# Queries and keys by seven half-size products, and one order for all block stages

## The chip, the cores and the metric

The kernel runs on one core of a Trainium2 chip. A core has a matrix engine (PE, with its weight loads listed apart as PEld), a vector engine (DVE), an activation engine (ACT), a third vector engine (POOL) and one that issues most of the DMAs (SP). Each takes its own instructions in the order in which they were written; semaphores tie them together. Matmul results land in PSUM, and DVE or ACT must read them out before the buffer can be used again.

The metric is the device time of one launch in microseconds, lower is better; the time of a kernel is the median of its runs.

## The reference

Two batches of 1024 tokens with 512 features, all fp32. After a layernorm there are two branches, and their product is added to the input.

```python
x = L0_attn_x                      # (2, 1024, 512)
xn = _layernorm(x, axis=-1)
# attention: 32 heads of 16, causal
q = (xn @ Wq.T + bq).reshape(b, l, h, hd).transpose(0, 2, 1, 3)
k = (xn @ Wk.T + bk).reshape(b, l, h, hd).transpose(0, 2, 1, 3)
v = (xn @ Wv.T + bv).reshape(b, l, h, hd).transpose(0, 2, 1, 3)
scores = jnp.einsum('bhqd,bhkd->bhqk', q, k) / math.sqrt(hd)
att = jax.nn.softmax(jnp.where(causal, scores, -jnp.inf), axis=-1)
s = jnp.einsum('bhqk,bhkd->bhqd', att, v).transpose(0, 2, 1, 3).reshape(b, l, d) @ Wo.T + bo
# gate: a base projection and two of eight rank-16 experts, chosen by a softmax
result = jnp.einsum('bnd,od->bno', xn, W_base) + b_base
g = _silu(result + delta * SCALING)
x = x + s * g
```

## The kernel before

The tokens of a batch are cut into two chunks of C = 512 (c = 0, 1), the features into KC = 4 blocks of 128 (oc). A *unit* (b, oc, c) is the attention of one chunk of queries for the eight heads of one block: 2 x 4 x 2 = 16 units. A unit of c = 0 has 5 steps and one of c = 1 has 13, since it looks back at the first chunk too: 144 steps in all, the list `plan`. The order of the units is by batch, block and chunk, with a few neighbours swapped, so that units of c = 0 often follow one another.

A step n writes, in this order: `scores(n)` (line 1218: matmuls of 32 rows side by side, then two exponentials of 128x1024 on ACT, line 1236), `values(n - 1)` (the product of the exponentials of the step before with v, line 1272), `masked(n)` (DVE multiplies the diagonal blocks of the exponentials by the causal mask), and `fill(n)`. At the end of a unit DVE copies two results, and `post` starts a chain of small DMAs and DVE operations (den, dens, rc, back, rb) that divides by the sums of the softmax.

`fill(n)` (line 1150) is a planner that runs while the program is written. All other work is a list of tasks, each with a due step, a cost in PE time (MM = 0.853 us by its own estimate, the time of 512 columns through 128 rows for all 128 outputs), conditions, and rooms (counts of free buffers) that it takes and frees. The planner takes matmul tasks in order of due step until the step has its even share of the remaining cost; tasks without matmuls (layernorm, sums, combining of weights) go where its estimate of DVE's time leaves room, or when they are due. So the order on every engine is settled before the kernel runs.

Products come in three forms. `matmul` (line 216) writes every product as four column groups of 32 outputs, which PE runs side by side; all of them are recorded at line 219.

- Queries and keys: `qk_task` (line 375) multiplies a block of weights (128 features out) with the 512 tokens of a chunk, four products of 128 rows and 512 columns for q and four for k. ACT reads q out twice (once for each parity of heads, line 388) and k once (line 402). The weights wq_sb and wk_sb are loaded once, 128 columns at a time, and stay in SBUF.
- Values, gate and output projections: `block_task` (line 515) computes a 512 by 512 product in blocks of 256, by seven block products in place of eight (Strassen's scheme in Winograd's form). For that `sums_task` (line 503) makes four sums of blocks of the tokens on DVE, and `combine_task` (line 459) four sums of blocks of the weights once, which go to DRAM (`kept`). The weight parts come back one by one into six buffers (`issue_parts`, tag wp). The ten such products are the `stages`, and stage k + 1 begins its sums only when stage k has ended.
- The first unit, the routing and the end have forms of their own.

PSUM has two buffers of tag mm for all these products, so a product can begin only when the one before the last has been read out. The sums of the tokens have one buffer (tag sums), taken from the beginning of a stage's sums to its end.

Of the kernel before, what the change touches and what calls it, by code (L numbers as in the profile page):

```python
# [8 lines left out]
F32 = mybir.dt.float32  # L9
# [8 lines left out]
P = 128  # L18
# [62 lines left out]
def direct(ctx, tc, sound, x, wq, wk, wv, wo, wb, wa, wg, wB, bq, bk, bv, bo, bb, out):  # L81
# [34 lines left out]
    def load_w(src, cols, name, o0=0):  # L116
        t = cst.tile([P, KC, cols], F32, name=name)
        nc.sync.dma_start(
            out=t, in_=src.rearrange("(kc p) o -> p kc o", p=P)[:, :, o0 : o0 + cols]
        )  # L120
        return t
# [15 lines left out]
    wq_sb = [load_w(wq, P, "wq_sb0")]  # L137
    wk_sb = [load_w(wk, P, "wk_sb0")]
    wv_sb = load_whole(wv, "wv")
    bv_sb = load_b(bv, "bv_sb")  # L140
    for oc in range(1, KC):
        wq_sb.append(load_w(wq, P, f"wq_sb{oc}", oc * P))
        wk_sb.append(load_w(wk, P, f"wk_sb{oc}", oc * P))
# [30 lines left out]
    bq_half = cst.tile([P, 2, KC], F32, name="bq_half")  # L174
    mhalf = cst.tile([P, 1], F32, name="mhalf")
# [130 lines left out]
    def first_task():  # L306

        xnT = sb.tile([P, KC, C], F32, tag="xnT", bufs=3, name="xnT_0_0")
        qT = sb.tile([P, 2, C], F32, tag="qT", bufs=3, name="qT_0_0_0")
        kT = sb.tile([P, C], F32, tag="kT", bufs=4, name="kT_0_0_0")  # L310
        xnTs[0, 0], qTs[0, 0, 0], kTs[0, 0, 0] = xnT, qT, kT
        pq = ps_av.tile([P, C], F32, tag="av", name="pq_first")
        pk = ps_av.tile([P, C], F32, tag="av", name="pk_first")

        def turn(t):
            pt = mm_tile("pt_x")
            for k in range(KC):
                nc.tensor.transpose(
                    pt[:, k * P : (k + 1) * P], first[t][:, k * P : (k + 1) * P], ident
                )  # L320
            nc.scalar.copy(
                xnT[:, :, t * P : (t + 1) * P], pt.rearrange("p (k t) -> p k t", k=KC)
            )
            turned_at[0, 0] = now[0] - 5

        def project_first(ps, w, t):
            cols = slice(t * P, (t + 1) * P)
            for k in range(KC):
                nc.tensor.matmul(  # L329
                    ps[:, cols], lhsT=w[:, k, :], rhs=xnT[:, k, cols], start=k == 0, stop=k == KC - 1  # L330
                )

        def queries(par):
            ve.tensor_scalar(
                qT[:, par], pq, bq_sb[:, 0:1], half[:, par : par + 1], ALU.add, ALU.mult
            )

        def keys(t0, t1):
            cols = slice(t0 * P, t1 * P)
            nc.scalar.activation(kT[:, cols], pk[:, cols], AF.Identity, bias=bk_sb[:, 0:1])  # L340

        def transform(t, s):
            normalize(first[t : t + 1], *s)
            turn(t)

        s0 = yield from statistics(first[0 : 1])
        s1 = yield from statistics(first[1 : 2])
        transform(0, s0)
        b_ps = mm_tile("b_ps")[:, 0 : 2 * KC]
        nc.tensor.transpose(b_ps, b_rows, ident[0 : 2 * KC, 0 : 2 * KC])  # L350
        nc.scalar.copy(b_sb, b_ps)
        s2 = yield from statistics(first[2 : 3])
        transform(1, s1)
        project_first(pq, wq_sb[0], 0)
        s3 = yield from statistics(first[3 : 4])
        transform(2, s2)
        project_first(pk, wk_sb[0], 0)
        transform(3, s3)
        room["x"] += 1
        keys(0, 1)  # L360
        project_first(pq, wq_sb[0], 1)
        project_first(pq, wq_sb[0], 2)
        project_first(pq, wq_sb[0], TT - 1)
        queries(0)
        queries(1)
        for par in range(2):
            ve.tensor_scalar(bq_half[:, par], bq_sb, half[:, par : par + 1], None, ALU.mult)
        project_first(pk, wk_sb[0], 1)
        yield 6 * MM
        project_first(pk, wk_sb[0], 2)  # L370
        project_first(pk, wk_sb[0], 3)
        keys(1, TT)
        yield 2 * MM

    def qk_task(b, oc, c):
# [4 lines left out]
        for k in range(KC):  # L380
            matmul(
                pq, lhsT=wq_sb[oc][:, k, :], rhs=xnT[:, k, :], start=k == 0, stop=k == KC - 1
# [12 lines left out]
        for k in range(KC):  # L395
            matmul(
                pk, lhsT=wk_sb[oc][:, k, :], rhs=xnT[:, k, :], start=k == 0, stop=k == KC - 1
# [5 lines left out]
        kTs[b, oc, c] = kT  # L403
        yield MM
# [25 lines left out]
    def v_task(b, i):  # L430
# [17 lines left out]
    PARTS = ("11", "t2", "21", "t3", "t1", "22", "t4")  # L448
    weights = {"v": (wv, bv_sb), "gate": (wb, bb_sb), "out": (wo, bo_sb)}
    stages = (  # L450
        [("v", 0, 1), ("gate", 0, 0), ("gate", 0, 1), ("v", 1, 0), ("out", 0, 0), ("v", 1, 1)]
        + [("out", 0, 1), ("gate", 1, 0), ("gate", 1, 1), ("out", 1, 0)]
    )
    parts = [(k, j) for k in range(len(stages)) for j in range(len(PARTS))]
    NWP = 6
    places, used, issued = {}, [0], [0]
    combined, kept_at, b_diff, sums, sums_at, issued_at, ended = {}, {}, {}, {}, {}, {}, [0]

    def combine_task(name, given=None):
# [5 lines left out]
        at = lambda i, j: w[:, 2 * i : 2 * i + 2, BK * j : BK * j + BK]  # L465
        s = sb.tile([P, 4, 2, BK], F32, tag="sums", bufs=1, name="wsum")
        ve.tensor_tensor(s[:, 0], at(0, 1), at(0, 0), ALU.subtract)
        ve.tensor_tensor(s[:, 1], at(1, 1), s[:, 0], ALU.subtract)
        yield WAIT
        ve.tensor_tensor(s[:, 2], at(1, 1), at(0, 1), ALU.subtract)  # L470
        ve.tensor_tensor(s[:, 3], at(1, 0), s[:, 1], ALU.subtract)
        kept = dram.tile([P, 4, 2, BK], F32, tag=f"kept_{name}", bufs=1, name="kept")
        nc.sync.dma_start(out=kept, in_=s)
# [4 lines left out]
        for _ in range(1 if given else 2):  # L478
            yield WAIT

    def issue_parts():
        while issued[0] < len(parts) and issued[0] - used[0] < NWP:
# [6 lines left out]
            if part[0] == "t":  # L489
                src = combined[name][:, int(part[1]) - 1]  # L490
# [6 lines left out]

    def tokens(k):
        name, b, c = stages[k]
# [3 lines left out]
    def sums_task(k):  # L503
        at = tokens(k)
        s = sb.tile([P, 4, 2, BK], F32, tag="sums", bufs=1, name="asum")
        ve.tensor_tensor(s[:, 0], at(1, 0), at(1, 1), ALU.add)
        yield PAUSE
        ve.tensor_tensor(s[:, 1], s[:, 0], at(0, 0), ALU.subtract)
        sums[k], sums_at[k] = s, now[0]
        yield PAUSE  # L510
        ve.tensor_tensor(s[:, 2], at(0, 0), at(1, 0), ALU.subtract)
        yield PAUSE
        ve.tensor_tensor(s[:, 3], at(0, 1), s[:, 1], ALU.subtract)

    def block_task(k, slot, final, more=None):

        name, b, c = stages[k]
        at, s = tokens(k), sums[k]
# [13 lines left out]
        def product(name, a):  # L532
            ps = mm_tile(name)
            part = k, used[0] - k * len(PARTS)
# [15 lines left out]
            used[0] += 1  # L550
            if not closes:
# [7 lines left out]
        add(s11, p1, like(s11, bias[:, 0:BK]))  # L559
        yield MM  # L560
        p6 = yield from product("p6", s[:, 1])
        add(s12, p6, s11)
        yield MM
        p2 = yield from product("p2", at(0, 1))
        add(s11, p2, s11)
        final(0, 0)
        yield MM
        p7 = yield from product("p7", s[:, 2])
# [4 lines left out]
        p5 = yield from product("p5", s[:, 0])  # L573
# [5 lines left out]
        p3 = yield from product("p3", s[:, 3])  # L579
# [11 lines left out]
        final(1, 0)  # L591
        ended[0] += 1
# [372 lines left out]
    units[-3], units[-2] = units[-2], units[-3]  # L965

    for n in (1, 2 * KC + 1):
# [8 lines left out]
    room = {"x": 1, "xnT": 2, "qT": 3, "kT": 4, "v": 3, "hl": 1, "hwT": 2, "g": 2, "sums": 1}  # L976
# [46 lines left out]
    def stage(task, what, due, cost, takes, uses, ready, frees=()):  # L1023

        k = stages.index(what)
        Task(
            due - 8 if k else -9, sums_task(k), 0.0, takes={"sums": 1},
            ready=lambda: ended[0] == k and ready(),
        )
        Task(  # L1030
            due, task(k), cost, takes=takes, uses=uses, frees={"sums": 1, **dict(frees)},
            ready=lambda: now[0] > sums_at.get(k, now[0]) and issued_at.get((k, 1), now[0]) < now[0],
        )

    tasks = []
    for b in range(NB):
        for c in range(NC):
# [11 lines left out]
            for oc in range(KC):  # L1049
                if oc or b or c:  # L1050
                    Task(
                        starts[b, oc, c] - 1, qk_task(b, oc, c), 8 * MM, takes={"qT": 1, "kT": 1},
                        uses=xn,
                        ready=lambda u=units[units.index((b, oc, c)) - 1], t=turned_: u in qk_begun
                        and t(),
                    )
            if not b and not c:
                room["v"] -= 1
                for t in range(TT):
# [5 lines left out]
                    3, combine_task("v", wv_sb), 0.0, after=5, takes={"sums": 1},  # L1065
                    frees={"sums": 1}, uses=[("xnT", "wv")],
                )
                for n, name in enumerate(("gate", "out")):
                    Task(
                        16 + n, combine_task(name), 0.0, after=9, takes={"sums": 1, "xnT": 1},  # L1070
                        frees={"sums": 1, "xnT": 1}, ready=lambda n=n: ended[0] > 0 and len(combined) > n,
                    )
            else:
                stage(values_task, ("v", b, c), s0 + (5 if c else 1), 14 * MM, {"v": 1}, xn, turned_)
            done = starts[b, KC - 1, c] + len(unit_steps(c))
            Task(
                done - (16 if (b, c) != (NB - 1, NC - 1) else 36), route_task(b, c), TT * KC * MM * (ER + E) / D, takes={"hl": 1}, uses=xn,
# [3 lines left out]
                done - (14 if (b, c) != (NB - 1, NC - 1) else 34), routed_task(b, c), 0.0, takes={"hwT": 1}, frees={"hl": 1},  # L1081
# [6 lines left out]
            if (b, c) != (NB - 1, NC - 1):  # L1088
                by = min(len(plan) - 3, done + (21 if c else 19 if b else 16))
# [4 lines left out]
            else:  # L1094
# [23 lines left out]
                )  # L1118
    tasks.sort(key=lambda x: x.due)
# [661 lines left out]
```

## Time and profile before

| | us |
|---|---|
| median of 3 runs | 611.37 (611.22 to 611.74) |
| profiled execution, whole | 612.12 |
| its span, first to last instruction | 610.4 |
| exponentials on ACT, line 1236, 288 of 1021 ns | 279.1 busy |
| pq and pk, 480 matmul records each, 592 ns | 56.6 and 56.6 busy |
| products of 256 columns, p<-wt,asum, 960 records, 379 ns | 58.0 busy |
| DVE's masks, 90 of 690 ns and 76 of 421 ns | 61.2 and 30.8 busy |
| ACT qT<-pq, 30 of 774 ns, and kT<-pk, 15 of 687 ns | 21.7 and 10.3 busy |
| bytes moved by DMA | 52.30 MB, mean 86 GB/s |

The granted clock of PE was 0.997. Busy times of PE count a stretch once even where four column groups run in it; the mean of one record is longer than the time until the next, because records overlap. So the price of a piece of work on PE is better read from the start of one step to the start of the next than from the records' means.

### The profile page before, as it was taken

Reading aid. Unit: us, or ns where it says so; the run is one execution under the profiler, and the core shown is the slowest. Engines: PE = TensorE matmul, PEld = TensorE weight load, DVE = VectorE, ACT = ScalarE, POOL = GpSimd, SP = SyncE. Lnnn points to the kernel's source line nnn. Section 1 sums busy time; section 2 is a strip of 40 time slices with the busy share of each in tenths; the row PEclk is TensorE's granted clock in tenths of the full one; section 3 lists DMA queues with packets and bytes.
Section 4 is the critical chain, followed back from the end, with each engine's and each line's share of the span. In section 5 each row is a group of like instructions: output and inputs, shape, how many; then the busy total and the mean of one; then the engine's idle time right before and its main releaser. Section 6 shows DMA issues by size and latency. Waiting matters only on the chain.

```text
span 610.4 us, 17914 instructions
## 1 busy us (share of the span) xinstructions
PE 599.4 (98%) x7991; PEld 265.4 (43%) x7991; DVE 346.2 (57%) x710; ACT 328.0 (54%) x381; POOL 8.9 (1%) x26
## 2 busy tenths in 40 slices
PE   8999999999999999999999999999999999999995
PEld 8335343423443244434344443452355444347662
DVE  4546664362298227856279644554349854766733
ACT  2435446566556655655545555446655655665351
POOL 2100000000000000000000000000000000000000
PEclk9999999999999999999999999999999999999998
DMA  9824315320521325025134121340112213401201
GB/s 270 180 70 141 113 55 175 119 91 19 130 59 46 106 54 124 22 72 183 46 100 133 39 73 57 103 124 4 35 37 74 58 40 101 163 19 41 72 20 57
DMA packets 47428, 52.30 MB, mean 86 GB/s; under 512 B 8056, under 2 KB 34688, under 8 KB 46960
## 3 DMA queue, kind: packets, MB, share of 16 engines
q1 hardware_dynamic: 47328, 51.08, 28.1%
q8 instruction: 64, 1.05, 0.7%
q14 instruction: 20, 0.16, 0.1%
q10 hardware_dynamic: 16, 0.00, 0.0%
HBM read 39.05 MB, written 12.03 MB: 84 GB/s over the span
## 4 chain that ended last, share of the span: by engine, by line
PE 95%; DVE 1%; DMA 1%; ACT 1%; issue 0%; SPq 0%; DVEq 0%
PE s L1227 25%; PE av L1272 23%; PE p L219 21%; PE pk L219 8%; PE pq L219 8%; PE pv L219 2%; PE ph L219 2%; PE po L219 2%; ACT pt L1236 1%; DMA x<-in_x_dram 1%; DMA dens<-den 1%; PE pq_first L329 1%; PE h L219 1%; PE pk_first L329 0%; DVE x L55 0%; DVE y L55 0%
## 5 line engine op out<-in xcount | busy, mean ns | idle before, releaser
L1236 ACT ACTIVATE pt<-s 128x1024 f32<-128x1024 f32 x288 | 279.1, 1021 | 210.6 <-PE s L1227 208.5
L1227 PE MATMUL s<-qT,kT 32*128 32x512 f32 (+3 forms) x1824 | 166.5, 464 | 0.1
L55 DVE TENSOR_TENSOR pt<-pt,causal 128x256 f32<-128x256 f32 (+1 forms) x166 | 92.1, 567 | 131.1 <-ACT pt L1236 130.9
L1272 PE MATMUL av<-pt,v 128*32 128x512 f32 (+3 forms) x1824 | 154.0, 443 | 0.6 <-DVE avs L55 0.6
L1227 PEld LDWEIGHTS s<-qT,kT 32*128 32x128 f32 x1824 | 72.9, 184 | 87.6 <-issue 40.5
L1272 PEld LDWEIGHTS av<-pt,v 128*32 128x32 f32 x1824 | 43.1, 109 | 89.4 <-issue 60.8
L219 PE MATMUL p<-wt,asum 128*32 128x256 f32 x960 | 58.0, 379 | 0.0
L219 PE MATMUL pk<-xnT,wk_sb 128*32 128x512 f32 x480 | 56.6, 592 | 0.0
L219 PE MATMUL pq<-xnT,wq_sb 128*32 128x512 f32 x480 | 56.6, 592 | 0.0
L219 PEld LDWEIGHTS p<-wt,asum 128*32 128x32 f32 x960 | 31.1, 110 | 27.8 <-issue 10.5
L55 DVE TENSOR_TENSOR g<-p,g 128x512 f32<-128x512 f32 x28 | 18.9, 687 | 21.7 <-PE p L219 21.4
L388 ACT ACTIVATE qT<-pq,bq_half,half 128x512 f32<-128x512 f32 x30 | 21.7, 774 | 14.4 <-PE pq L219 14.4
L219 PEld LDWEIGHTS pk<-xnT,wk_sb 128*32 128x32 f32 x480 | 15.5, 110 | 31.6 <-issue 31.1
L219 PEld LDWEIGHTS pq<-xnT,wq_sb 128*32 128x32 f32 x480 | 15.4, 110 | 29.1 <-issue 28.1
L219 PE MATMUL p<-w,xnT 128*32 128x256 f32 x448 | 26.7, 379 | 0.0
L55 DVE TENSOR_TENSOR v<-p,v 128x512 f32<-128x512 f32 x21 | 14.2, 689 | 19.3 <-PE p L219 19.1
L626 ACT ACTIVATE sg<-g 128x512 f32<-128x512 f32 x16 | 10.1, 630 | 21.1 <-DVE g L55 21.1
L219 PE MATMUL p<-w,asum 128*32 128x256 f32 x320 | 20.6, 379 | 0.0
L219 PEld LDWEIGHTS p<-w,xnT 128*32 128x32 f32 x448 | 14.4, 110 | 12.0 <-issue 4.8
L55 DVE TENSOR_TENSOR x<-p,x 128x512 f32<-128x512 f32 x21 | 14.1, 685 | 7.5 <-PE p L219 7.4
L219 PE MATMUL ph<-wag_sb,xnT 128*32 128x136 f32 x512 | 17.9, 280 | 0.3
L219 PEld LDWEIGHTS ph<-wag_sb,xnT 128*32 128x32 f32 x512 | 14.9, 110 | 7.1 <-issue 5.4
(122 smaller groups left out, 416.8 us busy)
## 6 DMA issues: line engine op xcount, KB each, us to landing
wt<-kept SPq DMA_DIRECT2D x40, 256.0 KB
x<-in_x_dram SPq DMA_DIRECT2D x16, 256.0 KB
scr<-sq SPq DMA_DIRECT2D x6, 512.0 KB
xnT<-scr SPq DMA_DIRECT2D x24, 128.0 KB
kept<-wsum SPq DMA_DIRECT2D x3, 1024.0 KB
w<-in_wb_dram SPq DMA_DIRECT2D x12, 256.0 KB
xr<-in_x_dram SPq DMA_DIRECT2D x12, 256.0 KB
out_dram<-x SPq DMA_DIRECT2D x12, 256.0 KB
```

Source lines behind the costliest of these rows:

```text
L55: return getattr(self.engine, name)(*args, **named)
L219: nc.tensor.matmul(o[j : j + 32], lhsT=lhsT[:, j : j + 32] if len(lhsT.shape) == 2 else lhsT[:, j // 32], rhs=rhs, start=start, stop=stop,)
L329: nc.tensor.matmul(ps[:, cols], lhsT=w[:, k, :], rhs=xnT[:, k, cols], start=k == 0, stop=k == KC - 1)
L388: nc.scalar.activation(qT[:, par], pq, AF.Identity, bias=bq_half[:, par, oc : oc + 1], scale=half[:, par : par + 1],)
L626: nc.scalar.activation(sg, g(i, j), AF.Tanh, scale=0.5)
L1227: nc.tensor.matmul(ss[s // 2][:, s % 2, col : col + w], lhsT=kT[rows, kt % TT * P : kt % TT * P + P], rhs=qTs[b, oc, c][rows, par, q0 : q0 ...
L1236: nc.scalar.activation(pt[:, 2 * pair : 2 * pair + 2], ss[pair], AF.Exp, scale=0.25)
L1272: nc.tensor.matmul(avs_now[par][32 * s : 32 * s + 32, q0 : q0 + w], lhsT=vs[b, kt][:, h * VS - HD * par : h * VS - HD * par + HP], rhs=pt[ ...
```

## The change

Thirteen of the sixteen units now get their queries and keys from `qk_blocks_task`. It puts the two weight blocks side by side as one 512 by 256 operand (128 outputs for q, 128 for k) and computes both by the same seven-product scheme: seven products with 256 rows and 256 tokens each, in place of eight with 128 rows and 512 tokens. The results are added up by DVE, eight operations of 128x256 a unit, in place of ACT's three reads; the biases enter there (`b_less` is bq - bk). ACT then makes the two parities of q from the finished tile, one step later.

The first unit and the two that follow it keep their old products. The weight blocks are loaded into two buffers in turn (`load_qk`), for each batch anew; `qk_weights_task` makes the weights' sums in the first batch, keeps them in DRAM, and fetches them in the second.

All block stages, those of q and k among them, stand in one list of groups and run in this order. Stages of one group use the same tokens and share one set of four token sums, which now have a buffer each; a sum for the next group may be written once the product that last reads the old one has been issued. The products of a stage come in another order (the two plain ones first), and `combine_task` writes the weights' sums in place. The due steps follow: no stage is due later than the one after it. Two neighbouring units of the first batch swap places, and routing and gate tasks are due at other steps.

```diff
+    def load_qk(oc):
+        t = sb.tile([P, 4 * KC, P], F32, tag="wqk", bufs=2, name=f"wqk{oc}")
+        for n, src in enumerate((wq, wk)):
+            nc.sync.dma_start(
+                out=t[:, n * KC : n * KC + KC],
+                in_=src.rearrange("(kc p) o -> p kc o", p=P)[:, :, oc * P : oc * P + P],
+            )
...
-    PARTS = ("11", "t2", "21", "t3", "t1", "22", "t4")
+    PARTS = ("11", "21", "t2", "t3", "t1", "22", "t4")
-    stages = (
-        [("v", 0, 1), ("gate", 0, 0), ("gate", 0, 1), ("v", 1, 0), ("out", 0, 0), ("v", 1, 1)]
-        + [("out", 0, 1), ("gate", 1, 0), ("gate", 1, 1), ("out", 1, 0)]
+    groups = (
+        [("v", 0, 1), ("qk", 0, 1, 1)],
+        [("gate", 0, 0), ("qk", 0, 0, 2), ("qk", 0, 0, 3)],
+        [("qk", 0, 1, 2), ("gate", 0, 1), ("qk", 0, 1, 3)],
+        [("v", 1, 0), ("qk", 1, 0, 0), ("qk", 1, 0, 1)],
+        [("out", 0, 0)],
+        [("qk", 1, 1, 0), ("v", 1, 1), ("qk", 1, 1, 1)],
+        [("out", 0, 1)],
+        [("qk", 1, 0, 2), ("qk", 1, 0, 3), ("gate", 1, 0)],
+        [("qk", 1, 1, 2), ("gate", 1, 1), ("qk", 1, 1, 3)],
+        [("out", 1, 0)],
     )
...
+    def qk_weights_task(n):
+        oc = n % KC
+        if n >= 2:
+            wqks.append(load_qk(oc))
+        w = wqks[n]
+        sums = w[:, 2 * KC :]
+        if n >= KC:
+            nc.sync.dma_start(out=sums, in_=qk_kept[oc])
+        else:
+            for _ in range(3 if n >= 2 else 0):
+                yield WAIT
+            yield from four_sums(
...
+            qk_kept[oc] = dram.tile([P, 2 * KC, P], F32, tag=f"kept_qk{oc}", bufs=1, name="kept")
+            nc.sync.dma_start(out=qk_kept[oc], in_=sums)
+        qk_ready[n] = now[0] + (2 if n >= KC else 0)
...
     def sums_task(k):
...
+        yield from ahead(4)
+        ve.tensor_tensor(place(2), at(0, 0), at(1, 0), ALU.subtract)
         yield PAUSE
+        ve.tensor_tensor(place(1), at(1, 1), s[2], ALU.subtract)
...
+        yield from ahead(5)
+        ve.tensor_tensor(place(0), s[1], at(0, 0), ALU.add)
         yield PAUSE
+        yield from ahead(6)
+        ve.tensor_tensor(place(3), at(0, 1), s[1], ALU.subtract)
...
+    def qk_blocks_task(k):
...
+        def product(name, a):
+            ps = mm_tile(name)[:, 0:BK]
+            n = place[PARTS[made[k]]]
+            for kc in range(2):
+                matmul(ps, lhsT=w[:, n + kc], rhs=a[:, kc], start=kc == 0, stop=kc == 1)
+            made[k] += 1
+            return ps
+
+        def add(o, ps, t, more=0.0):
+            ve.scalar_tensor_tensor(o, ps, more, t, ALU.add, ALU.add)
+
+        p1 = product("q1", at(0, 0))
+        ve.tensor_scalar(keys[0], p1, bias, None, ALU.add)
+        yield MM
+        add(q[0], product("q2", at(0, 1)), keys[0], less)
+        yield MM
+        s = yield from sums_of(k)
+        add(keys[0], product("q6", s[1]), keys[0])
+        yield MM
+        add(q[1], product("q7", s[2]), keys[0])
+        yield MM
+        p5 = product("q5", s[0])
+        add(keys[0], p5, keys[0])
+        add(keys[1], p5, q[1])
+        yield MM
+        add(keys[0], product("q3", s[3]), keys[0])
+        yield MM
+        add(q[1], product("q4", at(1, 1)), q[1], less)
+
+        def apart():
+            for par in (1, 0):
+                nc.scalar.activation(
+                    qT[:, par], qT[:, 0], AF.Copy, scale=half[:, par : par + 1]
+                )
+
+        later.append((now[0] + 1, apart))
...
-    units[-3], units[-2] = units[-2], units[-3]
-    for n in (1, 2 * KC + 1):
+    for n in range(1, 2 * KC * NB, 4):
         units[n], units[n + 1] = units[n + 1], units[n]
...
+    for k in reversed(range(len(stages) - 1)):
+        staged[k].due = min(staged[k].due, staged[k + 1].due)
+    for k, task in summed.items():
+        task.due = staged[k].due - int(staged[k].cost / 1.7) + 1 if k else -9
```

## The prediction

> **What bounds the kernel now.** I read the page's engine table first, then the chain of work that ended last, then the waits of PE, and then the timeline of PE step by step, because a busy share alone doesn't say what one step costs.
>
> ```profile
> span 610.4 us, 17914 instructions
> PE 599.4 (98%) x7991; PEld 265.4 (43%) x7991; DVE 346.2 (57%) x710; ACT 328.0 (54%) x381; POOL 8.9 (1%) x26
> ...
> PE 95%; DVE 1%; DMA 1%; ACT 1%; issue 0%; SPq 0%; DVEq 0%
> PE s L1227 25%; PE av L1272 23%; PE p L219 21%; PE pk L219 8%; PE pq L219 8%; PE pv L219 2%; PE ph L219 2%; PE po L219 2%; ACT pt L1236 1%; DMA x<-in_x_dram 1%; DMA dens<-den 1%; PE pq_first L329 1%; PE h L219 1%; PE pk_first L329 0%; DVE x L55 0%; DVE y L55 0%
> ```
>
> PE is on 95% of the chain and DVE on 1%, so a piece of PE work that goes away is worth its own length, as long as nothing takes its place. The target of the change, pk and pq, is 8% and 8% of it.
>
> ```profile
> PE warm L169 <- POOL ident masks.py:199: 1.4, 1, 1.4
> PE pt_x L318 <- DVE x L55: 0.8, 1, 0.8
> PE av L1272 <- DVE avs L55: 0.6, 1, 0.6
> PE pt_o L814 <- DVE y L55: 0.4, 1, 0.4
> PE po L219 <- ACT oT L845: 0.4, 1, 0.4
> ```
>
> These are PE's longest waits, all at the two ends: 3.6 us in sum. Between them PE never stands for DVE, ACT or a DMA.
>
> ```profile
> 144.98 1.07 PE L1272 MATMUL av<-pt,v 128*32 128x384 f32 x16
> 145.87 1.90 PE L219 MATMUL pk<-xnT,wk_sb 128*32 128x512 f32 x16
> 147.70 1.14 PE L1227 MATMUL s<-qT,kT 32*128 32x512 f32 x8
> 148.77 1.06 PE L1272 MATMUL av<-pt,v 128*32 128x512 f32 x8
> 149.65 1.91 PE L219 MATMUL p<-w,xnT 128*32 128x256 f32 x32
> 151.49 1.14 PE L1227 MATMUL s<-qT,kT 32*128 32x512 f32 x8
> ```
>
> This is PE's timeline (start, length, then the matmul). One attention step is scores, values, and a filling of other work. The score starts at 143.91, 147.70 and 151.49 give steps of 3.79 us; the chain in order of time has 1.72 us for a filling of two 512-column units of pk or pq and 1.73 us for the same amount in 256-column pieces of p. So 2.07 us of a step are attention and one unit of work (the planner's MM: four column groups side by side, 512 columns through 128 rows; 8 records, or 16 as two halves of 256) takes 0.858 us at 512 columns and 0.863 us in halves.
>
> [...]
>
> **The change, part by part.** The sums are made against the profiled execution: span 610.4, whole time 612.12, so 1.72 lies outside; the median of the runs is 611.37, 0.75 under it.
>
> Removed. Sixteen (batch, output block, chunk) units exist. The first keeps its own path, and the two that follow it in the new order keep `qk_task`. That leaves 13, each with 8 units of work: 13 x 2 x 3.43 us (the chain's 3.43 for a whole pq or pk) = 89.2 us of PE.
>
> Added on PE. Seven products of two 128-row halves by 256 tokens each: seven units of 0.863, 6.04 us; 13 times, 78.5 us. Net 10.7 us less PE work, all of it on the chain. Everything else PE does (attention, p, pv, ph, po) is the same instructions in another order.
>
> Moved off ACT. `qk_task` had two ACTIVATEs on qT (774 ns) and one on kT (687 ns): 2.24 us a unit. `apart` keeps two, from SBUF; the nearest row is sg<-g, 630 ns: 1.26. ACT gets 13 us lighter. Worth nothing: it has 46% idle, and a step of 3.79 us holds two exponentials of 1.02.
>
> Added on DVE. Eight operations of 256 columns a unit. At 421 ns (the row of the 128x256 mask) that is 3.37 us, 43.8 in all; the weights' sums, 16 operations, 6.7 us; b_less 0.2. The token sums stay at four per stage group, ten groups for ten stages. DVE goes from 346 to about 397 us, 66% of the span. As volume it is hidden behind PE. As order it isn't: DVE takes its instructions in turn, and a step's masks, which wait for the exponentials, stand ahead of the adds of that step's filling.
>
> ```profile
> 320.12 1.94 ACT L1236 ACTIVATE pt<-s 128x1024 f32<-128x1024 f32 x2 [2.72 <-PE s L1227]
> 320.26 0.69 DVE L55 TENSOR_TENSOR x<-x,xr 128x512 f32<-128x512 f32 x1
> 320.90 1.05 PE L219 MATMUL p<-w,asum 128*32 128x256 f32 x16
> 321.18 0.69 DVE L55 TENSOR_TENSOR pt<-pt,causal 128x512 f32<-128x512 f32 x1 [0.23 <-ACT pt L1236]
> 321.76 1.91 PE L219 MATMUL p<-wt,oT 128*32 128x256 f32 x32
> 322.09 0.69 DVE L55 TENSOR_TENSOR pt<-pt,causal 128x512 f32<-128x512 f32 x1 [0.22 <-ACT pt L1236]
> 322.70 0.68 DVE L55 TENSOR_TENSOR x<-p,x 128x512 f32<-128x512 f32 x1
> ```
>
> Here the filling begins at 320.90 and DVE is free of masks at 322.70. Put three q products into this filling: the first ends at 321.76, its add runs from 322.70 to about 323.12, and the third, which needs the first one's PSUM buffer (tag mm has two), could have begun at 322.62. It would stand for 0.5 us. With a filling of two products nobody waits: the next one starts 3.79 us later. With block products none waits even at three units, as one of them takes two. In a step without masks the add follows at once. So a stall needs three q products in one masked step. Masks: 166 operations, two a step, make 83 of 144 steps masked. Fillings: the tasks' costs, summed in their new order, are some 40 units of work by step 10 and 320 by the last of 144, so 280 in 134 steps, 2.1 a step; the sum reaches 94 at due step 34, 175 at 76, 217 at 93 and 290 at 129, close to that even line (90, 178, 213, 288); so twos rule and threes come where a due step presses. 91 products in some 43 fillings; I take 7 with three or more, 4 of them masked: 2.0 us. Bounds: nothing, and 18 us if each of the 26 masked ones stood 0.7 (the third waits for both masks and two adds).
>
> The masks in turn can be late: the steps of a c=0 unit carry up to 1.4 us of masks each, and 4.6 us a unit for the copies and the posts (the sum of the oT, avs, rb and rc rows over 15), 0.9 a step. Two q adds to three bring about 1.0. That is 3.3 of 3.79 us, and the page's DVE digits already reach 9 and 8 in such slices. I take 0.5 us in all; from nothing to 4.
>
> The weights. q and k blocks no longer stay in SBUF: eight loads of 512 KB in place of eight of 256 KB, four keeps and four fetches of 512 KB, 6 MB beside 52.3 MB that took 28% of the queue. They are asked for 2 or 3 steps (8 to 11 us) ahead of the first use, and at the 180 GB/s of the page's second slice a megabyte lands in 5.8 us. SP takes its DMAs in turn; a load that waits for PE to leave the old buffer holds up den, dens and back behind it, and DVE's reciprocal would wait for them. The page has one such wait now, 1.7 us for dens. I take nothing; bounds 0 and 3. At the start 1 MB less is ahead of the next x chunk, which nothing on the chain after 15 us waits for: nothing, at best -1.
>
> The fixed order. A stage can start only once the one ahead has ended, so a late sum or weight block leaves a step without filling. Now that happens twice (the score groups at 57.28 and 116.72 take 1.77 and 1.83 us in place of 1.14, as the exponentials aren't done): 0.7 us each. The fixed order takes away some choice, and the moved route tasks give some back, so I take the same number after as before: 0, bounds -1.4 (both go) and +4 (six more).
>
> Sum: 610.4 - 10.7 + 2.0 + 0.5 = 602.2; whole 603.9; on the median's level 603.2.
>
> **The rivals.** A: DVE becomes the bound wherever two c=0 units follow each other (a pair more of them than before). For: the adds above; against: half the steps have no masks and DVE catches up. At 0.07 to 0.17 us in each of the 40 steps of c=0 units the late masks cost 3 to 7 us in place of 0.5: 606 to 610, about 607.7. B, the slower side: the two PSUM buffers. If the planner gives q products in threes as a rule, the third stands 0.7 us behind masks and adds in each masked filling. 26 x 0.7 = 18 us against 10.7: 618.5 at most. It decides from 16 stalls of 0.7 on (10.7 / 0.7). For it: ACT emptied pq within 0.8 us with nothing ahead of it, and DVE won't; against: the even line of 2.1. C: nothing stands, the two unfilled steps go and the start gains: 10.7 + 1.4 + 1, to 598.3. That PE's work doesn't shrink as said I hold out: the p rows show the same form at the price used.
>
> **How the numbers follow.** Forecast (600 to 606) 0.63, A 0.17, B 0.12, C 0.08. The predicted time is the forecast's, 603.2. A and C lie with their larger part within 599.5 to 609.0, which leaves out B, the top of A and half of C: 0.2. What differs by under 0.2%, 1.2 us, can't be told from no change here. Faster: 0.63 + 0.08 + 0.14 of A = 0.85; same 0.03 from A's top; slower 0.12.
>
> **What would show it.** Right: 1456 records of 256 columns for the q products (13 x 7 x 16) near 379 ns, pq and pk down to two units' 64 each; steps of two q products at 3.80 us; PE's waits still only at the ends; DVE near 397 us; in the timeline the adds right behind the masks. Wrong: PE or PEld waiting for DVE on q products many times; steps of three products at over 4.7 us (2.07 + 3 x 0.863 = 4.66); scores of 1.7 us and more many times over, which would be unfilled steps; DVE's reciprocals waiting on dens for over 5 us.

## The result, and the profile after

The changed kernel takes 609.48 us (median of 10 runs, 608.45 to 610.68) beside 612.0 us for the kernel before in the same session (611.22 to 612.6). The ratio is 0.9959, with a 95% interval of 0.995 to 0.9969: faster by 2.5 us. The profiled execution took 610.35 us.

The page of the kernel after, the lines that answer to those shown of before (engines, PE's granted clock in 40 slices, the chain of waits by engine and by line):

```profile
span 608.5 us, 19376 instructions
PE 591.7 (97%) x8615; PEld 290.6 (48%) x8615; DVE 392.1 (64%) x831; ACT 319.1 (52%) x368; POOL 9.2 (2%) x26
...
PEclk9999999899999999999999999999999999999998
...
PE 86%; DVE 6%; DMA 4%; ACT 2%; SPq 1%; issue 1%; DVEq 0%
PE s L1375 23%; PE av L1420 21%; PE p L221 19%; PE q L221 11%; PE po L221 2%; PE pv L221 2%; PE ph L221 2%; ACT pt L1384 2%; DMA kept<-wqk 1%; PE pk L221 1%; PE pq L221 1%; DMA w_out<-in_wo_dram 1%; DMA x<-in_x_dram 1%; DMA dens<-den 1%; DVE pt L55 1%
```

PE is 7.7 us less busy, but its part of the chain fell from 95% to 86%. DVE, two DMAs that were not there (kept<-wqk and w_out<-in_wo_dram) and SP have taken the difference. The last of the 40 slices has a lower clock before, too; the other slice with an 8 is new.

PE's waits in the kernel after (who waited for whom: us in total, times, longest):

```profile
PE q L221 <- DVE kT L55: 3.9, 2, 3.0
PE warm L170 <- POOL ident masks.py:199: 1.4, 1, 1.4
PE pt_x L320 <- DVE x L55: 1.0, 1, 1.0
PE av L1420 <- DVE pt L55: 0.8, 2, 0.5
...
PE q L221 <- DVE g L55: 0.5, 1, 0.5
```

Before, all of PE's waits lay at the ends. Now it waits for DVE in the middle, and one wait of 3.0 us stands out.

**Where the gain went.** I took the start of every score group from the two timelines, and from each of the 143 steps between them subtracted 2.07 us of attention and its filling at the prices of the prediction (a matmul of 136 columns in proportion). What is left over is loss.

| part of the span | before | after | difference |
|---|---|---|---|
| first score group begins at | 15.04 | 15.48 | +0.4 |
| attention, 143 steps of 2.07 | 296.0 | 296.0 | 0 |
| work in the fillings of steps 0 to 142 | 276.3 | 265.6 | -10.7 |
| loss in steps 0 to 142 | 6.7 | 13.9 | +7.2 |
| last score group to the end | 16.3 | 17.5 | +1.2 |
| sum | 610.4 | 608.5 | -1.9 |

The 10.7 us were saved in full. Of the loss after, steps 18 and 19 have 5.2 us, step 15 has 0.8, steps 86, 113 and 115 have 2.1, steps 109 and 110 have 0.8. Of the 5.2 us, 0.3 aren't the stop's: step 19 is the second of two steps with 136-column products, which loses as much before (step 20), and it keeps them in the runs below where nothing stops. So the stall of steps 18 and 19 is 4.9 us. The losses of the two unfilled steps of before (8 and 22), 1.3 us, are gone.

The timeline of the kernel after around step 18 (start, length, engine, and in brackets how long the engine had stood and for what):

```profile
98.07 0.43 SPq L130 DMA_DIRECT2D w_out<-in_wo_dram  x1
...
101.49 1.91 PE L221 MATMUL q<-asum,wqk 128*32 128x256 f32 x32
103.33 1.14 PE L1375 MATMUL s<-qT,kT 32*128 32x512 f32 x8
104.40 1.07 PE L1420 MATMUL av<-pt,v 128*32 128x512 f32 x8
104.47 2.87 DVE L55 TENSOR_TENSOR w_out<-w_out 128x512 f32<-128x512 f32 x4 [3.01 <-DMA w_out<-in_wo_dram]
...
107.59 0.42 DVE L55 SCALAR_TENSOR_TENSOR kT<-q,kT 128x256 f32<-128x256 f32 x1
...
108.48 1.53 PE L221 MATMUL q<-xnT,wqk 128*32 128x256 f32 x16 [3.02 <-DVE kT L55]
109.71 1.66 PE L221 MATMUL ph<-wag_sb,xnT 128*32 128x136 f32 x24
```

It reads from the middle outwards. DVE reached the first of the four sums of w_out and stood 3.01 us for its load, which SP had issued only at 98.07; the sums then took 2.87 us. Behind them in DVE's order stood the adds for two q products that PE had long finished. PE wanted a third buffer and stood 3.02 us. But steps 18 and 19 lost 5.2 us, and the products after the stop look long: 1.53 us for 16 records that take 1.05 elsewhere. The windows of the same stretch (from:to, length, busy time of PE, PEld, DVE, ACT and POOL, then PE's granted clock, DMA's share and GB/s) say why; I set their bounds where the clock changes:

```profile
105.55:108.96 3.41, 0.48 (x11) 0.39 (x15) 3.34 (x8) 0.95 (x2) 0.00 (x0) 1.00 0.49 193
108.96:112.37 3.41, 3.41 (x44) 2.13 (x36) 2.69 (x5) 0.00 (x0) 0.00 (x0) 0.50 0.75 270
112.37:115.78 3.41, 3.31 (x68) 1.71 (x64) 0.00 (x0) 2.72 (x5) 0.00 (x0) 1.00 0.29 85
```

From just after the stop PE was granted half its clock for 3.41 us. The stop cost 3.0 us and the slow restart 1.8. It isn't a matter of the profiled run alone: the mean granted clock of the ten runs is 0.993 or 0.994, that of the kernel before 0.995 to 0.998 in the sessions that have it, and 3.41 us at half clock are 0.003 of the mean.

And why was w_out late? Before, it was asked for at 105.51 and summed at 118.01, 12.5 us later:

```profile
105.51 0.42 SPq L126 DMA_DIRECT2D w_out<-in_wo_dram  x1
...
118.01 0.69 DVE L55 TENSOR_TENSOR wsum<-w_out 128x512 f32<-128x512 f32 x1
```

Now the sums were due 3.4 us after the request, and the load landed 6.4 us after it. SP's own waits in that part of the span show what it stood for:

```profile
SPq L121 <- DMA kept<-wqk: 6.9, 1, 6.9
```

The load of the third weight block (line 121) overwrites the first one's buffer, from which its sums were still being written out. SP stood there from 76 to 83 us, with dens and, further back, hscr and w_out in its queue.

### The profile page after: what moved, and what is told of

It reads as the page before. It is cut to its first block, busy times and chain, and to the rows that moved or that the text cites. A ratio compares the mean times of both kernels' runs of the same rounds, so it can differ in the third digit from the quotient of the medians.

```text
span 608.5 us, 19376 instructions
## 1 busy us (share of the span) xinstructions
PE 591.7 (97%) x8615; PEld 290.6 (48%) x8615; DVE 392.1 (64%) x831; ACT 319.1 (52%) x368; POOL 9.2 (2%) x26
## 4 chain that ended last, share of the span: by engine, by line
PE 86%; DVE 6%; DMA 4%; ACT 2%; SPq 1%; issue 1%; DVEq 0%
PE s L1375 23%; PE av L1420 21%; PE p L221 19%; PE q L221 11%; PE po L221 2%; PE pv L221 2%; PE ph L221 2%; ACT pt L1384 2%; DMA kept<-wqk 1%; PE pk L221 1%; PE pq L221 1%; DMA w_out<-in_wo_dram 1%; DMA x<-in_x_dram 1%; DMA dens<-den 1%; DVE pt L55 1%
## 5 line engine op out<-in xcount | busy, mean ns | idle before, releaser
L55 DVE TENSOR_TENSOR pt<-pt,causal 128x512 f32<-128x512 f32 (+1 forms) x166 | 91.1, 566 | 78.9 <-ACT pt L1384 78.5
L221 PE MATMUL q<-asum,wqk 128*32 128x256 f32 x832 | 50.9, 379 | 0.2 <-DVE qT L55 0.2
L221 PE MATMUL q<-xnT,wqk 128*32 128x256 f32 x624 | 40.0, 383 | 4.4 <-DVE kT L55 3.9
L221 PEld LDWEIGHTS q<-asum,wqk 128*32 128x32 f32 x832 | 27.6, 110 | 23.2 <-issue 7.2
L221 PEld LDWEIGHTS q<-xnT,wqk 128*32 128x32 f32 x624 | 20.4, 110 | 25.6 <-issue 10.5
L55 DVE SCALAR_TENSOR_TENSOR kT<-q,kT 128x256 f32<-128x256 f32 x39 | 16.4, 422 | 16.1 <-PE q L221 15.0
L708 ACT ACTIVATE qT<-qT,half 128x512 f32<-128x512 f32 x26 | 18.8, 722 | 0.4
```

Source lines behind the costliest of these rows:

```text
L55: return getattr(self.engine, name)(*args, **named)
L221: nc.tensor.matmul(o[j : j + 32], lhsT=lhsT[:, j : j + 32] if len(lhsT.shape) == 2 else lhsT[:, j // 32], rhs=rhs, start=start, stop=stop,)
L708: nc.scalar.activation(qT[:, par], qT[:, 0], AF.Copy, scale=half[:, par : par + 1])
```

## The experiments

Theory 1: the loss is a chain of turns taken in order. SP stands, a load is late, DVE stands for it, the q adds stand behind DVE's wait, PE stops, and its clock drops. Theory 2, the rival: DVE simply has too much to do with the adds. Theory 3: the fixed order itself costs time.

**A step more for w_out**

```diff
-        for _ in range(0 if given else 2):
+        for _ in range(0 if given else 2 + (name == "out")):
             yield WAIT
```

> Theory 1 (the profile after: at step 18 DVE stands 3.0 us for w_out, whose load SP issued late, the q adds stand behind it, PE stops for 3.0 us and then runs at half clock): with one more step between the load of w_out and its sums DVE doesn't wait, step 18 goes from 7.97 to about 3.8 us and step 19 from 4.28 to 3.5, the granted clock stays at 1.00 there, and the time falls by 5 us, to about 604.5. Rival (DVE simply has too much to do with the q adds): the stall moves to the next step with q adds, and the time stays within 1.5 us of 609.5.

Measured: 606.6 us, ratio 0.9912 (0.9888 to 0.9937). The six runs fall in two groups, 604.06 to 604.99 and 608.21 to 608.43; the profiled one is of the first (604.99, span 603.3). In its trace step 18 has no loss, step 19 has its 0.3, and step 15 still has 0.9. The sums of w_out now come after the q adds in DVE's order, and DVE waits only 0.18 us for the load. So the chain is as theory 1 says, and theory 2's moving stall didn't come. What the other three runs lost isn't in a trace and stays open. That it didn't occur in the four runs with the next edit added hints at SP's queue, and no more.

**The third weight block two steps later**

```diff
                             and len(qk_ready) >= n
+                            and now[0] > qk_ready[n - 2] + 2
```

> The third weight block is asked for two steps later, so that SP doesn't stand 6.9 us for the keeping of the first block's sums (which still read that buffer) with dens, hscr, hwT and w_out queued behind it. If SP's stand is the root of it all (theory 1a): dens, hsq and the masks of step 15 are in time (0.8 us), w_out is asked for some us earlier, and step 18's stall goes too: about 604. If the load of w_out is late for its own reasons (its place in the plan two steps ahead, 1 MB): only step 15 gains, about 608.5.

Measured: 606.59 us, ratio 0.991 (0.9897 to 0.9922), between the two expectations. Step 15 has no loss: dens, hsq and with them the masks are in time. Step 18 still stops, 2.04 us in place of 3.02, in the profiled run, which at 608.76 was the longest of five. The load of w_out was issued at 97.07 in place of 98.07, so SP's stand was only 1.0 us of its lateness; the rest is its place in the plan and in SP's order (hscr and hwT still go ahead of it). The granted clock of the profiled run was 0.993, that of the other four (606.14 to 607.15 us) 0.995 to 0.997. That would fit a stop there without a half clock behind it, or none, but no trace of them shows it.

**Both edits**

> Both edits. If they mend one and the same stall: as the better of the two, about 604. If step 15's late masks are a loss of their own: another 0.8 us, about 603.5. The stalls of three-product fillings (2.1 us in steps 86, 113, 115) stay in every theory.

Measured: 604.38 us (603.82 to 604.9), ratio 0.9872 (0.9858 to 0.9886). The timeline of this kernel at the same place:

```profile
97.23 0.43 SPq L130 DMA_DIRECT2D w_out<-in_wo_dram  x1
...
103.41 0.42 DVE L55 SCALAR_TENSOR_TENSOR kT<-q,kT 128x256 f32<-128x256 f32 x1
103.62 1.06 PE L1421 MATMUL av<-pt,v 128*32 128x512 f32 x8
103.74 0.41 DVE L55 SCALAR_TENSOR_TENSOR kT<-q,qT 128x256 f32<-128x256 f32 x1
...
104.07 0.41 DVE L55 SCALAR_TENSOR_TENSOR kT<-q,kT 128x256 f32<-128x256 f32 x1
104.40 2.86 DVE L55 TENSOR_TENSOR w_out<-w_out 128x512 f32<-128x512 f32 x4
104.50 1.05 PE L221 MATMUL q<-xnT,wqk 128*32 128x256 f32 x16
```

The load is issued hardly earlier (97.23 and 98.07), but the same four sums now come after the q adds in DVE's order. They need not wait, nothing waits for them, and the third product follows the values at once. Two lines of the plan are worth 5.1 us. Which of the two expectations holds, the total can't tell: the loss in the steps is 0.8 us less than in the trace with the first edit alone (8.4 and 9.2), step 15's, but the first score group began 0.5 us later.

**Eight products in the same order.** The computation is the same; each of the thirteen units takes its queries and keys by `qk_task`'s products, read out by ACT.

```diff
-        p1 = product("q1", at(0, 0))
...
+        for half_, name in enumerate(("pq", "pk")):
+            ps = mm_tile(name)
+            for kc in range(KC):
+                matmul(
+                    ps, lhsT=w[:, half_ * KC + kc], rhs=xnT[:, kc], start=kc == 0, stop=kc == KC - 1
+                )
...
-                        qk_blocks_task, ("qk", b, c, oc), starts[b, oc, c] - 2, 7 * MM, takes, xn,
+                        qk_blocks_task, ("qk", b, c, oc), starts[b, oc, c] - 2, 8 * MM, takes, xn,
```

> The order, the weight loads and the weights' sums of the changed kernel, but the thirteen units by eight products of 512 columns, read out by ACT. If the loss is made by the q adds that stand behind DVE's waits, the stalls of steps 18 and 19 (5.2 us) and of the three-product fillings (2.1 us) go and 10.7 us of work come back: 609.5 + 10.7 - 7.3, about 613. If the fixed order costs time by itself: the stalls stay and it is about 620.

Measured: 616.31 us, ratio 1.0074 (1.0062 to 1.0086), between the two. The stops of step 18 and of the three-product fillings are gone. The wait for w_out is not: DVE stands for it even longer, and PE goes on.

```profile
104.22 2.87 DVE L55 TENSOR_TENSOR w_out<-w_out 128x512 f32<-128x512 f32 x4 [4.71 <-DMA w_out<-in_wo_dram]
105.21 1.07 PE L1399 MATMUL av<-pt,v 128*32 128x512 f32 x8
106.09 1.90 PE L221 MATMUL pk<-xnT,wqk 128*32 128x512 f32 x16
```

So it is the q adds that carry DVE's waits to PE, and not the late load by itself. But step 15 loses 1.7 us here (PE stood 1.4 for late masks) and step 111 loses 2.2. The order costs something of its own.

**Eight products with both edits**

> Both edits, and the thirteen units by eight products of 512 columns read out by ACT. If PE alone bounds the kernel once the waits are gone, seven products are worth their 10.7 us less the 2.1 of the three-product fillings: 604.4 + 8.6, about 613, which is the kernel before and 1 us. If the order or the added loads cost PE time that the seven products hide: above 615.

Measured: 614.76 us, ratio 1.0039 (1.0025 to 1.0053). Step 15's loss is gone here too; step 111 keeps its 2.2, where PE waits 1.1 us for DVE's adds of the gate. So the order and the added loads, with the same products, are 2.8 us slower than the kernel before, and most of that is one step. In this order, with both edits, seven products are 10.4 us faster than eight (604.38 and 614.76).

**At most two q products in a masked step**

```diff
+        def room_left():
+            while (
+                in_fill.get(now[0], 0) >= 2 and 0 <= now[0] < len(plan) and mask_time(now[0])
+                and staged[k].due > now[0] + 1
+            ):
+                yield WAIT
...
         yield MM
+        yield from room_left()
```

> On the kernel with both edits, the planner gives a masked step no third q product unless one is due. If the third product's wait for the first one's PSUM buffer behind the masks is what steps 86, 113 and 115 lose (0.4, 0.7 and 1.1 us), that goes: 604.4 - 2.1, about 602.3, with PE's waits for DVE on q products under 0.5 us. If the loss belongs to the steps (DVE late whatever PE is given), the waits move to other products and the time stays near 604.4.

Measured: 602.51 us (602.36 to 603.11), ratio 0.9843 (0.983 to 0.9857), faster than both kernels of the case. PE's longest waits are back at the ends and at the scores, as this view of its waits shows:

```profile
PE warm L170 <- POOL ident masks.py:199: 1.4, 1, 1.4
PE s L1390 <- ACT pt L1399: 0.7, 3, 0.3
PE pt_y L980 <- DVE olast L55: 0.6, 1, 0.6
```

Step by step the sum is less neat than its total: steps 113 and 115 lose nothing now (1.8 us), nor do 109 and 110, where the new plan has other work (0.8); step 86 keeps its 0.4, as ph now stands behind the same adds; and the rule empties step 93, whose scores in step 94 then wait for ACT (1.4 lost). That the third product's wait was the loss of steps 113 and 115 is shown; that the total met the forecast is in part chance.

**DVE held on purpose.** The results are the same; the added operations write a scratch tile.

```diff
+        p6 = product("q6", s[1])
+        for n in range({("qk", 1, 0, 0): 13, ("qk", 1, 0, 2): 11}.get(stages[k], 0)):
+            nc.vector.tensor_tensor(idle, p6 if not n else idle, idle, ALU.mult)
-        add(keys[0], product("q6", s[1]), keys[0])
+        add(keys[0], p6, keys[0])
```

> Both edits, and idle DVE operations of 128x256 put ahead of one q add: 13 of them (some 5 us) in a step where the next product then stands about 3 us, 11 (some 4.5 us) in another where it stands about 1.3. If a long stop of PE is followed by work at half clock, as the profile after shows behind step 18, the first one costs its stall and about 2 us more, with a granted clock near 0.5 for some 4 us, and the second its stall alone. If the half clock at step 18 came from something else, each costs its stall alone: about 604.4 + 4.3 in that case, 606.5 + 4.3 in the other.

Measured: 612.34 us, one run. The stops were longer than meant, 3.56 and 2.64 us, since the idle operations started 456 ns apart where I had counted some 410. Their steps lost 5.43 and 2.85 us. The kernel with both edits, the two stops and 1.9 us of half clock make 612.5. The windows around the first stop, then around the second, the latter counted on in pieces of 3.413 us from the clock's change at 278.05, since the clock doesn't change there:

```profile
271.23:274.64 3.41, 0.11 (x4) 0.14 (x8) 3.09 (x9) 0.78 (x1) 0.00 (x0) 1.00 0.00 0
274.64:278.05 3.41, 3.41 (x32) 1.69 (x31) 2.37 (x7) 0.00 (x0) 0.00 (x0) 0.50 0.28 115
...
411.17:414.58 3.41, 2.22 (x28) 0.68 (x24) 3.17 (x8) 1.94 (x2) 0.00 (x0) 1.00 0.00 0
414.58:417.99 3.41, 1.96 (x24) 0.81 (x24) 2.69 (x10) 0.23 (x1) 0.00 (x0) 1.00 0.00 0
417.99:421.40 3.41, 3.41 (x52) 1.50 (x48) 1.83 (x9) 1.94 (x2) 0.00 (x0) 1.00 0.00 0
```

A stop made elsewhere brings the half clock as well, and 1.9 us on top of it. The second stop, longer than that of step 18 in the kernel with the later load, brought little but itself (2.85 us lost for 2.64).

## Why the prediction was wrong

It said 603.2 us, 599.5 to 609.0, from a gain of 8.2; the gain was 2.5. By its own steps:

- **PE's work: right.** There are 832 + 624 = 1456 q records with means of 379 and 383 ns, steps with two q products take 3.79 to 3.80 us, and the fillings shrank by 10.7 us.
- **DVE's and ACT's volume: right.** DVE 392 us against 397, ACT 319 against 315 (the parities of q took 722 ns each, not 630), and neither mattered as volume.
- **The third product behind the masks: right in mechanism; the sum is in part luck.** 2.0 us forecast from four stalls of 0.5; 2.1 found in three, of 0.4, 0.7 and 1.1 (in step 113 one of the three is a block product), and the 1.8 of two of them gone when no third product was given. Rival B was this mechanism in every masked step; the plan seldom gives threes.
- **Late masks: 0.5 forecast, 1.5 found** in steps 15 and 109 to 110, within the bound of 4. Step 15's 0.8 is a late dens, shown by the two experiments with the later load. That of 109 (routing operations and copies ahead of the mask on DVE) was only read from the trace.
- **The weights: this step failed.** "I take nothing; bounds 0 and 3": it was 4.9 us at steps 18 and 19, and 0.8 more by way of dens: 5.7 together, as much as the gain fell short, since the other terms' misses nearly cancel. I had priced the new loads by their bytes and by the lead that their own tasks have, and they were indeed in time. The sentence that SP's load would hold up den, dens and back behind it was right, and I gave it no price. What I left out is the old load of w_out, which the change moves earlier in the plan and past a crowded SP queue, while the sums that need it keep a distance of two steps. And I had no price for what stands behind DVE's wait: q products, which ACT used to read out and which now depend on DVE. The way to PE is that of rival B, the two PSUM buffers, with a late load in place of the masks. The bound of 3 was reached by the stop alone (3.02); the half clock behind it went beyond.
- **The fixed order: nothing forecast** (-1.4 to +4). By eight products with both edits it is +2.8; with seven products both steps of before that went unfilled are gone (1.3 us). The end has 1.2 us more in the kernel after, and between 0.7 and 1.4 in all its variants: step 142 has no filling and the last scores wait for ACT. That it comes from the planner's last shares was not tried.
- **The start: noise.** Step 1 begins between 21.31 and 22.25 us in the nine traces.

With the two plan edits the kernel stands at 604.4, and with the third at 602.5: the forecast's mechanism was there, under a stall that it had put at zero.

## What to carry to other kernels

When an edit moves the reading of PSUM from one engine to another, list what that engine waits for, not only how busy it is: a DMA wait in its queue can become a wait of PE, as the one of 3.0 us did here, once both buffers are full. And when the order of tasks changes, check each load whose consumer has a fixed distance in steps, the old ones too, by when its issue leaves the queue rather than by when it was planned.

## What the runs showed of the hardware

A stop of PE can cost more than its length. Behind stops of 3.02, 2.04 and 3.56 us the granted clock fell to 0.5 for 3.41 us, and the steps lost 1.8, 1.8 and 1.9 us beyond the stop (half of 3.41 us would be 1.7); behind one of 2.64 us it stayed at 1.00.

The times at which the clock changes say more. In the kernel after they are 6.56, 108.96, 112.38 and 603.89 us, and the stretches between them are 30, 1 and 144 times 3.413 us; in the kernel before they are 6.01 and 606.76 us, 176 times that apart. So I divided the span into cells of this length that begin with a change. The windows shown of the kernel after and of the last experiment are such cells; these are the two of the kernel with the later load, behind whose stop of 2.04 us the clock fell:

```profile
103.79:107.20 3.41, 1.37 (x16) 0.41 (x20) 3.34 (x8) 1.94 (x2) 0.00 (x0) 1.00 0.24 101
107.20:110.61 3.41, 3.41 (x43) 2.24 (x36) 3.34 (x8) 0.00 (x0) 0.00 (x0) 0.50 0.90 344
```

In the cells ahead of a half clock PE was busy for 0.48, 1.37 and 0.11 us. The stop of 2.64 us lies across two cells, with 2.22 and 1.96 us of PE's work, and no half clock follows. Of the kernels before and after I counted the cells of the whole span from the first change on. The half clock at the end of each begins behind a cell with 0.18 and 0.51 us of PE's work, and every cell ahead of full clock had 2.41 us or more. No cell of these lies between 1.37 and 1.96 us, so where the border is was not measured. In these traces, then, the half clock goes with how little PE did in one cell. A rule of the stop's length alone doesn't fit: 2.04 us brought the half clock and 2.64 us didn't. The cells lay elsewhere against the kernel in the two traces (from 6.01 us on before, from 6.56 us on after). Why the clock falls no run shows.
